# Edge values by four quarter-array products, and the picks spread over the groups anew

## Chip, cores and metric

The kernel runs on one core of one Trainium2 chip. The metric is device time of one execution in microseconds (us). Before the change it is 1745.33 us, median of three runs (1743.85 to 1745.64).

## The reference, cut to what matters

A graph with 6250 nodes and 206250 edges (sorted by destination), 64 features, 4 heads of 16:

```
Q, K, V = x @ Wq.T + bq, x @ Wk.T + bk, x @ Wv.T + bv      # per node
Ee      = edge_attr @ We.T + be                            # per edge
score   = (K[src] * Q[dst] / sqrt(16) * Ee).sum(per head)
score   = exp(clip(score, -5, 5))
out     = layernorm(x + segment_sum(V[src] * score, dst))
```

## The kernel before, in words

The edges are cut into 1612 tiles of 128, eight tiles to a **group** (202 groups, the last one of four tiles). A first part makes the K|V table (`kv_tab`) and the Q table in memory. Then one loop of 203 iterations, `for g in range(NG + 1)` (L867), handles the groups in a software pipeline whose order is written out by hand (the scheduler is off); each engine runs its own instructions in that order. What an iteration g does, by engine:

- **TensorE**, in this order: the edge product of group g + 3 (`edges`, L686), the **pick** matmuls of its share of blocks (`picks`, L654), four transposes that turn the terms of group g + 1 back to edges-by-features (`turn`, L713), two query products of group g + 2 (`queries`, L697), and, in every second iteration, 16 **sums** (`sums`, L782), which add the messages of a step of two groups by destination. All but the transposes are issued through `product` (L684), so they share that line in the profile and are told apart by their tiles: `ee` edge product, `pick` picks, `qq` queries, `room` sums.
- **ScalarE**: bias added to the edge product (`biased`, L695), exponentials (L741), two passes that make the query one-hots (L243, L249), parts of the messages (`keep`, L765).
- **VectorE**: one-hots of the picks (`hots`, L644), scores (L732 to L737), messages (L753), what `keep` left (`take`, L770), one-hots of the sums (L724), `add` (L805 and L811), which adds a finished step's sums to the result's rows, and the terms of group g + 2 (L708).
- **GpSimd**: one indirect DMA per tile that gathers the 128 source rows of `kv_tab` (L260), up to four steps ahead of use.
- **SyncE**'s queue: edge features, keys, query windows, source lists.

A **pick** stands in for gathers: the rows of four tiles at a time (a batch) are selected out of all nodes by one-hot matmuls. A batch takes 25 blocks of three matmuls (`parts` against `hot`, 512 columns), accumulated in a PSUM bank, and then a closing piece (`picked_kv`, L669: one product with the bias and four full-precision products). Two groups per batch have two of their tiles picked and not gathered. `first_unit(g)` (L74) says with which block an iteration begins: 25 blocks per three iterations from the sixth on, shared 9, 8, 8. From it follow when a batch starts (`BEGIN`), is complete (`READY`) and which groups it serves (`PICKED`, four and five groups after it is ready). `LAST`, the number of batches, is 62, so 248 tiles are picked, 40 are made by the first part, and 1324 are gathered. The picks end eleven groups before the end.

The **edge product** (L686): eight tiles lie as four pairs, `ET[g]` is 128 partitions (two tiles' 64 features) by four blocks of 128 edges. The weight `we_sb` is 128 x 128 with `We` transposed in the two diagonal quarters and zeros in the other two. One full-precision product of 512 columns fills the PSUM bank `ee`. The queries of a group are already two products with 64 output rows each, into the two partition halves of `qq`.

PSUM has eight banks here: `still` (constants), `room` (sums in 192 of 512 columns, and 64 for their total), two for picks, `ee`, `qq`, two `qe`. Messages go into `qe`. `add` stands amid the iteration (behind `take(g, 0)`) for the late steps, and at its end for all others. Most of a step's 16 sums can lie between the pairs of pick blocks, the rest behind the queries.

Of the kernel before, what the change touches and what calls it, by code (L numbers as in the profile page):

```python
# [7 lines left out]
F32 = mybir.dt.float32  # L8
# [3 lines left out]
AF = mybir.ActivationFunctionType  # L12
# [3 lines left out]
P = 128  # L16
N = 6250
C = 64
# [4 lines left out]
G = 8  # L23
# [3 lines left out]
NS = len(STEPS)  # L27
NR2 = 112
ONES = NS - 8
# [23 lines left out]
def tiles_of(g):  # L53
    return min(G, T - g * G)
# [6 lines left out]
def groups_of(s):  # L61
    return range(STEPS[s][0], STEPS[s][0] + STEPS[s][1])
# [5 lines left out]
UNITS = NB // 2  # L68
MOST = 5
LEAD = 6  # L70
# [2 lines left out]

def first_unit(g):  # L74

    return UNITS * ((g - LEAD) // 3) + (0, 9, 17)[(g - LEAD) % 3]


def when(k):
# [48 lines left out]
def tile_gnn(ctx: ExitStack, tc: tile.TileContext, x, x_blocks, by_rows, xT, wT, bias, beT, weT, eT, src, src_rows, dst,  # L128
             dst_rows, out):
    nc = tc.nc  # L130
# [29 lines left out]
    ident = consts.tile([P, P], F32, name="ident")  # L160
# [18 lines left out]
    we_sb = consts.tile([P, 2 * C], F32, name="we_sb")  # L179
# [5 lines left out]
    be_col = consts.tile([P, 1], F32, name="be_col")  # L185
# [11 lines left out]
    ET, QW, at = {}, {}, {}  # L197
    SRC, FROM, ODD, KB, TO = ({} for _ in range(5))
# [398 lines left out]
    with tc.If(rv == 0) as branch:  # L597

        with tc.tile_pool(name="work", bufs=2) as work, \
# [7 lines left out]
            nc.tensor.transpose(col, row_b[:, 0:1].to_broadcast([P, P]), ident_b)  # L607
            nc.tensor.transpose(still[:, C:C + NB].bitcast(BF16), half_b[:2 * NB].to_broadcast([2 * NB, P]),
                                ident_b[:2 * NB, :2 * NB])
            room = fixed.tile([P, 4 * P], F32, name="room")  # L610
            pa = room[:, :3 * C]
            sum_ = room[:, 3 * C:4 * C]
            px = [fixed.tile([P, 4 * P], F32, name=f"pick{k}") for k in range(2)]
            xs = [accp.tile([P, 4 * P], F32, name=f"x{k}") for k in range(2)]
            ee = fixed.tile([P, G // 2, P], F32, name="ee")
            qq = fixed.tile([P, G // 2, P], F32, name="qq")
            qe = [fixed.tile([P, G, C], F32, name=f"qe{k}") for k in range(2)]

# [30 lines left out]
            def by_two(todo):  # L649

                blocks = [(k, w, w + 1 == end) for k, end in todo for w in range(k, end)]
                return [blocks[i:i + 2] for i in range(0, len(blocks), 2)]
# [30 lines left out]
            def product(*aps, **kw):  # L683
                mark.append(nc.tensor.matmul(*aps, **kw))  # L684

            def edges(g):  # L686

                n = tiles_of(g) // 2
                product(ee[:, :n, :], we_sb, ET[g][:, :n, :], start=True, stop=True)

            def biased(g):

                n = tiles_of(g) // 2
                EB[g] = work.tile([P, G // 2, P], F32, name="eb")
                nc.scalar.activation(EB[g][:, :n], ee[:, :n], AF.Identity, bias=be_col)  # L695

            def queries(g):  # L697

                n = tiles_of(g)
                for u in range(2):  # L700
                    product(qq[u * C:(u + 1) * C, :n // 2, :], QW[g], TO[g][:, u:n:2, :],
                                     start=True, stop=True)

            def terms(g):
# [4 lines left out]

            def turn(g):  # L710

                for u in range(tiles_of(g) // 2):
                    nc.tensor.transpose(qe[g % 2][:, 2 * u:2 * u + 2, :].rearrange("p j c -> p (j c)"),  # L713
                                        TERM[g][:, u, :], ident)

            def onehot_edges(s):

# [59 lines left out]

            def pa_of(s):

                return {NS - 3: px[0][:, :3 * C], NS - 2: px[1][:, :C], NS - 1: ee[:, 0, :C]}.get(s, pa)  # L780

            def sums(s, lo=0, hi=2 * G):  # L782
                n = tiles_in(s)
                for j in range(lo, min(hi, n)):
                    product(pa_of(s), (OF if s >= WHOLE else OH)[s][:, j, :],
                            MSG[s][:, j].rearrange("p i c -> p (i c)") if s < WHOLE else MSG[s][:, j, :],
                            start=j == 0, stop=j == n - 1,
                                     skip_group_check=True)
# [78 lines left out]
            for g in range(NG + 1):  # L867
                now, before = g < NG, g > 0
                todo, ahead = pieces(g), pieces(g + 1)
                going, where = [], []  # L870
                if g < 2:
                    going = alone(lots(4)[2 * g:2 * g + 2])
                elif now and step_of[g] + KVB - 1 < NS:
                    going = lots(step_of[g] + KVB - 1)
                    going = alone(going[:2] if g == groups_of(step_of[g])[0] else going[2:])
                if g % LG == 0 and g + 3 * LG < NG:
                    fetch_edges(g // LG + 3)
                if g + 1 in BEGIN[1:]:
                    fetch_sources(BEGIN.index(g + 1) + 1, work)
                if g + 4 < NG:  # L880
                    fetch_queries(g + 4)
                if g % 2 == 0 and g + 6 < NG:
                    fetch_keys(g + 6, work)
                done = [s for s in range(NS) if groups_of(s)[-1] + 2 == g]
                parted = now and step_of[g] < WHOLE
                fetch_blocks(g)
                where.append(mark[-1])
                if g + 3 < NG:
                    edges(g + 3)
                if now:  # L890
                    products(g)
                    weigh(g)
                if g + 3 < NG:
                    biased(g + 3)
                for mc in ahead[:1]:
                    hots(*mc)
                if now:
                    message(g)
                if g + 4 < NG:
                    onehot_rows(g + 4, work.tile([3 * W, G, P], BF16, name="to", bufs=4))  # L900
                if parted:
                    keep(g, 0)
                for mc in ahead[1:]:
                    hots(*mc)
                if parted:
                    take(g, 0)
                if g > groups_of(ONES - 1)[-1]:
                    for s in done:
                        add(s)
                if g - 1 in READY:  # L910
                    picked(READY.index(g - 1))
                if g - 2 in READY:
                    picked_kv(READY.index(g - 2))
                    place_kv(READY.index(g - 2))
                where.append(mark[-1])
                summed = 0
                for i, some in enumerate(by_two(todo)):
                    picks(some)
                    if i and parted and g - 1 in ends:
                        sums(ends[g - 1], summed, summed + 4)  # L920
                        summed += 4
                    where.append(mark[-1])
                if g + 1 < NG:
                    turn(g + 1)
                if g + 2 < NG:
                    queries(g + 2)
                where.append(mark[-1])
                if g - 1 in ends and now:
                    sums(ends[g - 1], summed)
                if g + 4 < NG:  # L930
                    onehot_rows_rest(g + 4)
                if parted:
                    keep(g, 1)
                if g in BEGIN:
                    sources(BEGIN.index(g) + 1, *from_odd())
                for i, lot in enumerate(going):
                    gather((lot, where[i * len(where) // len(going)]))
                for h in ([g] if g < NG - 3 else []) + ([g + 1] if NG - 4 <= g < NG - 1 else []):
                    if h not in ends:
                        continue  # L940
                    s = ends[h]
                    t0 = STEPS[s][0] * G
                    for t in range(t0, t0 + tiles_in(s)):
                        if t and t % KEYS == 0:
                            keys(t)
                    onehot_edges(s)
                    if s >= WHOLE:
                        widen(s)
                if parted:
                    take(g, 1)  # L950
                if g <= groups_of(ONES - 1)[-1]:
                    for s in done:
                        add(s)
                if g + 2 < NG:
                    terms(g + 2)
                if done:

                    while closed < B - 2 and due[closed] <= done[-1] + 1:
                        spreads(closed)
                        closed += 1  # L960
                    if closed in BATCHES and closed > scaled:
                        roots(scaled, closed)
                        scales(scaled, closed)
                        scaled = closed
                    for _ in range(3):
                        if normed < scaled:
                            norm(normed)
                            normed += 1
# [178 lines left out]
```

## Time and profile before

| | before |
|---|---|
| median of three runs | 1745.33 us |
| profiled execution, own time | 1744.26 us |
| its span, first to last instruction | 1742.4 us |
| PE (matmul) busy | 1661.7 us, 95% |
| DVE (VectorE) busy | 1569.6 us, 90% |
| ACT (ScalarE) busy | 918.4 us, 53% |
| POOL (GpSimd) busy | 1310.5 us, 75% |
| pick matmuls (512 columns) | 4495 recorded, 1052.4 us |
| edge products | 404 records, 227.4 us |
| sums | 1592 recorded, 200.2 us |
| gathers | 1324, 1270.7 us |
| mean granted TensorE clock | 0.974 |

How to read the rows: a group's row has line, engine, operation, output<-inputs, shapes and count, then busy time in us and the mean of one in ns, then the idle time of the engine just before these instructions and what ended it. In rows in order of time, the first number is the start from the span's beginning, the second how long the merged instructions took. A matmul's record is longer than its distance to the next one, because matmuls are pipelined and the ends are modelled; so starts are compared with starts here. PEld is the weight load. POOL's busy time leaves out what its queue needs between two gathers. The chain that ended last is followed back from the last instruction, at each step to what released it.

### The profile page before, as it was taken

What the parts mean: (1) busy time and instruction counts of PE and PEld (TensorE: products, weight loads), DVE (VectorE), ACT (ScalarE), POOL (GpSimd) and SP (SyncE); (2) the same over time, 40 slices, a digit from 0 to 9 for tenths busy, and PEclk for the clock granted to TensorE, in tenths of its full rate; (3) what the DMA queues carried; (4) which work ended last, traced back from release to release, by engine and by line L of the source; (5) the groups of instructions that cost most, each with busy time, mean ns of one, the idle gap of its engine ahead of it and who ended that gap; (6) DMA issues with size and microseconds to landing.
All of it is one profiled execution on the core that took longest, in us unless ns stands there. A gap on an engine that the chain in (4) does not pass through costs nothing.

```text
span 1742.4 us, 26109 instructions
## 1 busy us (share of the span) xinstructions
PE 1661.7 (95%) x8456; PEld 881.2 (51%) x8611; DVE 1569.6 (90%) x2637; ACT 918.4 (53%) x1507; POOL 1310.5 (75%) x1374
## 2 busy tenths in 40 slices
PE   7779999999999999999999999999999999999964
PEld 6435555555555555555555555555555555555533
DVE  5689999999999999999999999999999999999976
ACT  3655555545555555555555555555555555555553
POOL 7777777777777777777777777777777777777775
PEclk9879999999999999999999999999999999999985
DMA  6744444343443443434434344344343443434331
GB/s 191 246 120 133 112 118 116 102 121 101 117 120 103 120 113 104 122 108 121 121 102 120 104 114 118 99 120 117 106 132 97 120 113 103 121 107 125 108 89 47
DMA packets 115144, 203.65 MB, mean 117 GB/s; under 512 B 55475, under 2 KB 56223, under 8 KB 114885
## 3 DMA queue, kind: packets, MB, share of 16 engines
q1 hardware_dynamic: 70914, 112.68, 21.7%
q0 software_dynamic: 43648, 88.17, 19.5%
q10 hardware_dynamic: 436, 1.04, 0.3%
q8 instruction: 69, 1.13, 0.3%
q14 instruction: 77, 0.63, 0.1%
HBM read 194.18 MB, written 7.59 MB: 116 GB/s over the span
## 4 chain that ended last, share of the span: by engine, by line
PE 90%; DMA 3%; DVE 2%; issue 2%; ACT 2%; POOL 1%; SPq 0%; POOLq 0%; DVEq 0%; ACTq 0%
PE pick L684 62%; PE ee L684 11%; PE room L684 7%; PE qe L713 5%; PE qq L684 4%; DMA kv<-kv_tab,src_i 2%; POOL kv L260 1%; PE ps L462 1%; DMA wkv<-in_wT 1%; DMA et<-in_eT 0%; PE pv L542 0%; DVE score L735 0%; DVE prod L732 0%; DVE term L708 0%; ACT eb L695 0%
## 5 line engine op out<-in xcount | busy, mean ns | idle before, releaser
L260 POOL DMA_INDIRECT kv<-kv_tab,src_i x1324 | 1270.7, 960 | 403.5 <-issue 197.1
L684 PE MATMUL pick<-hot,parts 128*128 128x512 bf16 x4495 | 1052.4, 379 | 8.3 <-issue 0.2
L684 PEld LDWEIGHTS <-parts 128*128 128x128 bf16 x4650 | 451.9, 98 | 527.1 <-issue 73.3
L644 DVE TENSOR_TENSOR hot<-from,still 128x2560 bf16<-128x2560 bf16 x366 | 460.0, 1257 | 0.0
L741 ACT ACTIVATE score<-score 128x32 f32<-128x32 f32 x202 | 46.3, 229 | 732.7 <-DVE score L737 732.7
L765 ACT ACTIVATE msg<-qe 128x512 bf16<-128x512 f32 x400 | 238.6, 596 | 35.8 <-DVE qe L753 26.9
L684 PE MATMUL ee<-et,we_sb 128*128 128x512 f32 x404 | 227.4, 645 | 7.1 <-ACT eb L695 6.1
L249 ACT ACTIVATE to<-to,one_p 126x1024 bf16<-126x1024 bf16 x198 | 226.5, 1144 | 0.0
L243 ACT ACTIVATE to<-kb,minus_row 126x1024 bf16<-126x1024 uint8 x198 | 224.6, 1134 | 0.0
L684 PE MATMUL room<-msg,of 128*128 128x192 bf16 x1592 | 200.2, 252 | 17.6 <-DVE y L811 11.3
L684 PEld LDWEIGHTS <-of 128*128 128x128 bf16 x1600 | 142.8, 100 | 109.5 <-DVE y L811 19.9
L770 DVE TENSOR_TENSOR msg<-qe,msg 128x512 bf16<-128x512 f32 x200 | 136.9, 685 | 67.4 <-ACT msg L765 61.3
L708 DVE TENSOR_TENSOR term<-eb,qq 128x512 f32<-128x512 f32 x202 | 137.0, 678 | 20.1 <-PE qq L684 15.8
L770 DVE TENSOR_TENSOR qe<-qe,msg 128x512 f32<-128x512 f32 x200 | 138.2, 691 | 18.2 <-ACT msg L765 18.2
L732 DVE TENSOR_TENSOR prod<-kv,qe 128x512 f32<-128x512 f32 x202 | 137.3, 680 | 8.2 <-DMA kv<-kv_tab,src_i 3.4
L735 DVE TENSOR_REDUCE score<-prod 128x32 f32<-128x512 f32 x202 | 138.3, 685 | 7.0
L713 PE MATMUL qe<-ident,term 128*128 128x128 f32 x806 | 126.2, 281 | 18.7 <-DVE term L708 18.7
L753 DVE TENSOR_TENSOR qe<-kv,score 128x512 f32<-128x512 f32 x200 | 139.0, 695 | 4.1 <-ACT score L741 4.1
L695 ACT ACTIVATE eb<-ee,be_col 128x512 f32<-128x512 f32 x202 | 135.1, 669 | 4.6 <-PE ee L684 4.6
L724 DVE TENSOR_TENSOR of<-still,key 128x2048 bf16<-128x2048 bf16 (+2 forms) x105 | 122.7, 1169 | 0.2
L713 PEld LDWEIGHTS qe<-ident,term 128*128 128x128 f32 x806 | 97.3, 144 | 49.8 <-DVE term L708 29.9
L684 PE MATMUL qq<-to,qw 126*64 126x512 bf16 x396 | 82.4, 413 | 0.0
(138 smaller groups left out, 855.5 us busy)
## 6 DMA issues: line engine op xcount, KB each, us to landing
et<-in_eT SPq DMA_DIRECT2D x100, 512.0 KB
kb<-key_tab SPq DMA_DIRECT2D x101, 252.0 KB
kv<-kv_tab,src_i POOLq DMA_INDIRECT x1324
srcs<-in_src_rows SPq DMA_DIRECT2D x62, 256.0 KB
qw<-q_tab SPq DMA_DIRECT2D x202, 15.8 KB
kv_tab<-kv_sb SPq DMA_DIRECT2D x4, 640.0 KB
q_tab<-q SPq DMA_DIRECT2D x5, 480.0 KB
y<-in_x_blocks SPq DMA_DIRECT2D x2, 512.0 KB
```

Source lines behind the costliest of these rows:

```text
L243: nc.scalar.activation(TO[g][:, :n, :], KB.pop(g)[:, :n * P].rearrange("p (j e) -> p j e", j=n), AF.Square, bias=minus_row3[:3 * W])
L249: nc.scalar.activation(TO[g][:, :n, :], TO[g][:, :n, :], AF.Relu, bias=one_p[:3 * W], scale=-1.0)
L260: return nc.gpsimd.indirect_dma_start(out=kv_of(g)[:, j, :], out_offset=None, in_=kv_tab[:, :], in_offset=bass.IndirectOffsetOnAxis(ap=src ...
L644: nc.vector.tensor_tensor(HOT[k][:, :hi - lo].rearrange("p b (a c) -> p b a c", c=2), pairs(FROM[m])[:, None].to_broadcast(shape), block2[ ...
L684: mark.append(nc.tensor.matmul(*aps, **kw))
L708: nc.vector.tensor_mul(TERM[g][:, :n], EB.pop(g)[:, :n], qq[:, :n])
L713: nc.tensor.transpose(qe[g % 2][:, 2 * u:2 * u + 2, :].rearrange("p j c -> p (j c)"), TERM[g][:, u, :], ident)
L732: nc.vector.tensor_mul(prod[:, :n, :], kv_of(g)[:, :n, :C], qe[g % 2][:, :n, :])
L735: nc.vector.tensor_reduce(score, prod[:, :n, :].rearrange("p g (h d) -> p g h d", h=H), axis=AX.X, op=OP.add)
L753: nc.vector.tensor_mul(to.rearrange("p g (h d) -> p g h d", h=H), kv_of(g)[:, :n, C:].rearrange("p g (h d) -> p g h d", h=H), SCORE[g][:, ...
L765: nc.scalar.activation(part, left, AF.Copy)
L770: nc.vector.tensor_sub(left if i == 0 else part_of(g, 2)[1], left, part)
```

## The change

1. **Edges.** The product over the whole array becomes four full-precision products of 64 input rows by 64 output rows, 256 columns each, one per quarter of the array: partition half `r` of `ET[g]` (one tile of each pair), tile pairs of half `u`. Output partitions are half `u`, and the two `r` go to two banks. The order is u = 0: r = 0, 1; then u = 1: r = 0, 1. The zero quarters of `we_sb` are no longer used here.
2. **Banks.** `room` becomes two banks: `ee` takes the first 256 columns of both, the sums and their total the second half of the first one. So edge values and sums share a bank, and `add` stands amid the iteration for all steps; the sums all come behind the queries, none between picks.
3. **What follows from the layout.** The bias activation reads both banks and writes the blocks interleaved; the queries take a contiguous half of the one-hots instead of every second tile; a transpose writes tiles k and k + half instead of two neighbours.
4. **Picks.** 35 blocks per four iterations. `LAST` becomes 65, so 260 tiles are picked and 1312 gathered.

```diff
 def first_unit(g):
-    return UNITS * ((g - LEAD) // 3) + (0, 9, 17)[(g - LEAD) % 3]
+    return (g - LEAD) * 35 // 4
...
-            room = fixed.tile([P, 4 * P], F32, name="room")
-            pa = room[:, :3 * C]
-            sum_ = room[:, 3 * C:4 * C]
+            room = fixed.tile([P, 2, 4 * P], F32, name="room")
+            ee = room[:, :, :2 * P].rearrange("p r (i e) -> p r i e", e=P)
+            pa = room[:, 0, 2 * P:2 * P + 3 * C]
+            sum_ = room[:, 0, 2 * P + 3 * C:2 * P + 4 * C]
...
-            ee = fixed.tile([P, G // 2, P], F32, name="ee")
...
             def edges(g):
-                n = tiles_of(g) // 2
-                product(ee[:, :n, :], we_sb, ET[g][:, :n, :], start=True, stop=True)
+                n = tiles_of(g) // 4
+                for u in range(2):
+                    for r in range(2):
+                        rows = slice(r * C, (r + 1) * C)
+                        product(ee[u * C:(u + 1) * C, r, :n, :], we_sb[rows, rows],
+                                ET[g][rows, u * n:(u + 1) * n, :], start=True, stop=True)
...
-                nc.scalar.activation(EB[g][:, :n], ee[:, :n], AF.Identity, bias=be_col)
+                nc.scalar.activation(EB[g][:, :n].rearrange("p (i r) e -> p r i e", r=2),
+                                     ee[:, :, :n // 2], AF.Identity, bias=be_col)
...
-                    product(qq[u * C:(u + 1) * C, :n // 2, :], QW[g], TO[g][:, u:n:2, :],
+                    product(qq[u * C:(u + 1) * C, :n // 2, :], QW[g],
+                                     TO[g][:, u * n // 2:(u + 1) * n // 2, :],
                                      start=True, stop=True)
...
-                for u in range(tiles_of(g) // 2):
-                    nc.tensor.transpose(qe[g % 2][:, 2 * u:2 * u + 2, :].rearrange("p j c -> p (j c)"),
-                                        TERM[g][:, u, :], ident)
+                half = tiles_of(g) // 2
+                for k in range(half):
+                    nc.tensor.transpose(qe[g % 2][:, k:k + half + 1:half, :], TERM[g][:, k, :], ident)
...
-                if g > groups_of(ONES - 1)[-1]:
-                    for s in done:
-                        add(s)
+                for s in done:
+                    add(s)
...
-                summed = 0
-                for i, some in enumerate(by_two(todo)):
+                for some in by_two(todo):
                     picks(some)
-                    if i and parted and g - 1 in ends:
-                        sums(ends[g - 1], summed, summed + 4)
-                        summed += 4
...
-                    sums(ends[g - 1], summed)
+                    sums(ends[g - 1])
...
-                if g <= groups_of(ONES - 1)[-1]:
-                    for s in done:
-                        add(s)
```

More of the change, by code (lines that the diff above doesn't have):

```diff
@@ L778, in pa_of, with sums @@
             def pa_of(s):
-                return {NS - 3: px[0][:, :3 * C], NS - 2: px[1][:, :C], NS - 1: ee[:, 0, :C]}.get(s, pa)
-            def sums(s, lo=0, hi=2 * G):
+                return {NS - 3: px[0][:, :3 * C], NS - 2: px[1][:, :C], NS - 1: room[:, 1, 2 * P:2 * P + C]}.get(s, pa)
+            def sums(s):
                 n = tiles_in(s)
-                for j in range(lo, min(hi, n)):
+                for j in range(n):
                     product(pa_of(s), (OF if s >= WHOLE else OH)[s][:, j, :],
```

## The prediction, written before the changed kernel had run

> **What bounds the kernel now.** I read the page first, then the busy time of each engine by stretches of the span, then the chain of work that ended last, cut at the same places, and last single rows of TensorE and VectorE in time.
>
> ```profile
> span 1742.4 us, 26109 instructions
> 210.00:1650.00 1440.00, 1432.45 (x7456) 742.11 (x7599) 1341.46 (x2163) 765.76 (x1218) 1093.12 (x1139) 1.00 0.41 113
> 1655.00:1732.00 77.00, 45.91 (x218) 27.39 (x217) 57.52 (x118) 36.70 (x61) 56.49 (x60) 0.72 0.28 75
> ```
>
> The columns of the last two rows are the stretch, its length, then busy time of PE, PEld, DVE, ACT and POOL, the granted clock and DMA. From 210 to 1650 us TensorE is busy 1432.45 of 1440 us: the main loop is TensorE's sum and nothing else. VectorE follows with 93%. From 1655 to 1732, the last eleven groups, which have no picks, TensorE is busy only 45.91 of 77. The chain says the same:
>
> ```profile
> by line: PE pick L684 69.9%; PE ee L684 12.0%; PE room L684 8.3%; PE qe L713 5.2%; PE qq L684 4.0%; issue 0.5%
> ...
> 1671.10 3.57 DMA kv<-kv_tab,src_i
> 1678.59 3.02 DMA kv<-kv_tab,src_i
> 1707.30 2.53 DMA kv<-kv_tab,src_i
> 1728.53 3.02 DMA kv<-kv_tab,src_i
> ```
>
> The first row is the chain between 210 and 1650: TensorE alone, 12% of it (some 173 us) edge products. The other rows are pieces after 1655: there the chain runs over gathers that landed late. GpSimd is the second limit:
>
> ```profile
> L260 POOL DMA_INDIRECT kv<-kv_tab,src_i x1139 | 1093.9, 960 | 347.1 <-issue 159.4 <-PE pick L684 63.4 <-DMA kv<-kv_tab,src_i 43.6
> L260 POOL DMA_INDIRECT kv<-kv_tab,src_i x1324: 940/944/1463, 55.6 to 1728.5; - x190
> ```
>
> In the same 1440 us it issued 1139 gathers, busy 1093.9 and idle 347.1: 1441.0 us, so 1.265 us each, the 0.30 us between two of them included, without a pause. Its last gather starts at 1728.5 and the span ends 14 us later. So TensorE sets the time up to about 1655, and GpSimd's queue, never empty, sets the last 75 us. A gain has to come in both, a loss needs only one.
>
> **The picks.** 25 blocks per three groups become 35 per four: 8.33 become 8.75 per group. In the planner's numbers 62 batches become 65, so 75 more blocks of three matmuls, three more batch ends, and 12 fewer gathers.
>
> ```profile
> 898.59 0.59 PE L684 MATMUL ee<-et,we_sb 128*128 128x512 f32 x1
> 899.11 0.39 PE L684 MATMUL pick<-bkv_p,ones_b 3*128 3x512 bf16 x1
> 899.43 1.16 PE L684 MATMUL pick<-w,x 128*128 128x128 f32 x8
> 900.42 0.38 PE L684 MATMUL pick<-hot,parts 128*128 128x512 bf16 x1
> ...
> 907.80 0.62 PE L684 MATMUL ee<-et,we_sb 128*128 128x512 f32 x1
> 908.26 0.59 PE L684 MATMUL ee<-et,we_sb 128*128 128x512 f32 x1
> 908.69 5.34 PE L684 MATMUL pick<-hot,parts 128*128 128x512 bf16 x24
> ```
>
> 24 pick matmuls take 5.34 us, the last one 0.38: (5.34 - 0.38) / 23 = 0.2157 us from one to the next. 75 x 3 x 0.2157 = 48.5 us; a batch end is 899.11 to 900.42 = 1.31 us, three are 3.9. TensorE gains **52.4 us** of work. GpSimd loses 12 x 1.265 = **15.2 us**.
>
> VectorE builds the blocks:
>
> ```profile
> L644 DVE TENSOR_TENSOR hot<-from,still 128x2560 bf16<-128x2560 bf16 x183 | 270.7, 1479 | 0.0
> ```
>
> 1.479 us for five blocks is 0.296 each, 22 us for 75. It lies behind TensorE, since VectorE has 98.5 us idle in the stretch of 1440; without that cover it would cost its 22.
>
> **The edge product.** This decides. One full-precision product is two matmul records, each with a weight load of its own, of 512 columns each. Now it becomes four products of 64 rows by 64 columns, 256 columns wide, so eight records of half the length.
>
> ```profile
> 913.87 0.60 PE L713 MATMUL qe<-ident,term 128*128 128x128 f32 x4
> 914.40 0.41 PE L684 MATMUL qq<-to,qw 126*64 126x512 bf16 x2
> 914.74 0.70 PE L684 MATMUL ee<-et,we_sb 128*128 128x512 f32 x1
> 915.27 0.59 PE L684 MATMUL ee<-et,we_sb 128*128 128x512 f32 x1
> 915.70 0.38 PE L684 MATMUL pick<-hot,parts 128*128 128x512 bf16 x1
> ...
> 914.74 0.19 PEld L684 LDWEIGHTS ee<-et,we_sb 128*128 128x128 f32 x1 [0.23 <-issue]
> 914.85 0.19 PEld L684 LDWEIGHTS ee<-et,we_sb 128*128 128x128 f32 x1
> ```
>
> Before, behind the queries: 914.74 to 915.70 = 0.96 us. Before, behind the sums (rows of 907.80 to 908.69 above): 0.89. A record streams 915.27 to 915.70 = 0.43 us; half as many columns I take at 0.214. (The eight 128-column records above, 899.43 to 900.42, come to 0.12 each, so a length does scale with columns.) The first of 914.74 took 0.53 because its weights, 0.11 from one load to the next, weren't there; 64 columns I take at 0.05. Three more rows price a change of the array's division: the query pair (64 columns each) starts 0.20 after the last transpose (913.87 + 3 x 0.11 = 914.20) where a step is 0.11, so 0.09; from the pair to the edge product, 914.40 + 0.216 = 914.62 to 914.74, is 0.12; and 898.59 to 899.11 is 0.52 instead of 0.43 ahead of the 3-row product, so 0.09.
>
> How do the eight overlap? The two query products, on two column halves, do run at once:
>
> ```profile
> L684 PE MATMUL qq<-to,qw 126*64 126x512 bf16 x394 | 81.9, 413 | 0.0
> ```
>
> Busy 81.9 us for 197 pairs is 0.416 a pair, as long as one of them. But each query product is a single record. An edge quarter is two records on the same quarter, and the rows show the second (915.27) starting only when the first has streamed. TensorE starts its matmuls in the order of the program in every row I read; if the waiting second record holds up the next quarter's first one, only neighbours overlap: quarter 1's second beside quarter 2's first, and so on. Eight records then take **five** lengths, not two: 5 x 0.214 = 1.07 us, where the old product streams four (2 x 0.43 = 0.86).
>
> The Trainium skill, page "TensorE: Matmul & The Clock Gate", section "The mechanism", states that matmuls start and end in program order and that only weight loads are pulled ahead; by that rule five lengths are right and the three later weight loads are hidden, which gives 1853 us in place of my sum below. No run here shows full-precision products in quarters.
>
> So after the queries: 0.05 + 1.07 + 0.12 to the picks' full array = 1.24, +0.28. After the sums another change, 0.10, is added: 1.34, +0.45. The groups alternate: +0.37. If the three later quarters each wait 0.05 for weights it is +0.53. I take the middle, **+0.45 us** for each of some 190 groups up to 1655: **+85 us**. Bounds: two lengths with everything at once (-0.28) and eight lengths with nothing at once (+1.01, from +0.37 + 3 x 0.214); both ends are rivals.
>
> **What costs nothing.**
>
> ```profile
> L695 ACT ACTIVATE eb<-ee,be_col 128x512 f32<-128x512 f32 x202 | 135.1, 669 | 4.6 <-PE ee L684 4.6
> ```
>
> The activation that adds the bias reads two banks and writes interleaved blocks of 128; ScalarE is busy 765.76 of 1440, so its cover is 674 us, and a 10% longer eb (0.07 of 0.67 us) would be 14 us behind it. Transposes into every second 64 columns, queries from a contiguous half, the terms: same elements, taken at nothing, between -0.05 and +0.05 a group (10 us) if addressing matters. The sums, now whole behind the queries instead of partly between picks, are the same 16 matmuls.
>
> **The new wait.** The edge values share a bank with the sums, so every second edge product waits for VectorE's add of the group before; behind it on TensorE stands everything.
>
> ```profile
> 912.84 0.69 DVE L770 TENSOR_TENSOR qe<-qe,msg 128x512 f32<-128x512 f32 x1
> ...
> 915.17 0.35 DVE L805 TENSOR_REDUCE room<-room 128x64 f32<-128x192 f32 x1
> 915.56 0.28 DVE L811 SCALAR_TENSOR_TENSOR y<-room,above,y 128x64 f32<-128x64 f32 x1
> 915.76 0.28 DVE L811 SCALAR_TENSOR_TENSOR y<-room,below,y 128x64 f32<-128x64 f32 x1
> ```
>
> The add takes 915.17 to 916.04 = 0.87 us; moved behind the subtraction that ends at 913.53 it would end at 914.40, and this edge product, after one of the shortest groups, starts at 914.74. 0.3 us are spare, more when TensorE is later: nothing in the forecast; between 0 and 0.2 us for at most 50 groups, 0 to 10 us, where TensorE is quicker.
>
> **The sum**, against the profiled execution (1744.26 us, span 1742.4): +52.4 + 85 = 137. The tail gives back: with TensorE this much later the gathers are there, and the 77 us fall towards VectorE's 57.5 plus some waits; I take -15 (-5 to -20). 1744.3 + 137.4 - 15 = 1866.7. The median of the runs lies 1.1 above the profiled one: **1868 us**, own range 1840 to 1892.
>
> **Rivals.**
> *Faster: all four quarters at once.* If TensorE holds a waiting record per quarter, the eight take two lengths: 0.05 + 0.43 + 0.12 = 0.60 after queries (-0.36), 0.70 after sums (-0.19), mean -0.275 x 190 = -52 us. That cancels the picks' +52.4, TensorE reaches the tail as now, GpSimd is 15.2 earlier: 1745.3 - 15 = 1730, up to 1740 with the new wait. It decides in favour below about -0.26 a group. For it: the query pair; against it: each quarter has two records. The Trainium skill, page "TensorEngine Tiling (Array Packing)", section "Key Properties", has tiles operating independently, loads and matmuls in parallel; by that rule this rival holds. Chance 0.30.
> *Between.* Four lengths (one more overlap): +0.16 x 190 = 30, + 52 - 15: 1813, some 1790 to 1839. 0.08.
> *The quarters take turns*, so the change doesn't do what it says: +1.01 x 190 = 192, + 52 - 15: 1975. Nothing in the rows shows two row halves at once. 0.10.
>
> **How the numbers follow.** Forecast 0.52, the others as given. Faster by over 0.2% (about what a measurement here tells from no change) needs under 1741.8: 0.28, the rival's 0.30 less 0.02 for a new wait that eats it. Within 0.2%: 0.02. Slower: 0.52 + 0.08 + 0.10 = 0.70. The range 1725 to 1892 takes in the fast rival, the one between and the forecast, 0.90 less some 0.07 for edges that I mis-size; only the turns lie outside.
>
> **What would show it.** In the changed profile, the start of a quarter's first record to the next picks: 1.2 to 1.5 us confirms, 0.6 refutes, 1.9 means turns. In single rows, does quarter 2 start with quarter 1's first or second record? TensorE busy near 100% of the loop confirms that it bounds; gathers with pauses would show GpSimd relieved. A group of pick matmuls above 0.2157 apart, or edge products idle before an add on VectorE, would make the sum wrong elsewhere.

## The result, and the profile after

The changed kernel takes 1740.78 us, median of nine runs (1739.53 to 1741.76), beside 1744.51 us (1742.83 to 1746.65) for nine runs of the kernel before: ratio 0.9975, 95% interval 0.9965 to 0.9985. So it is slightly faster, where the forecast was 1868 us, slower by 7%. It is 11 us above the figure of the rival "all four quarters at once", and it lies inside the wide range of 1725 to 1892 us only because that range took in this rival. The profiled execution takes 1741.34 us.

The page of after, first line, and the busy times by stretch (columns as before: stretch, length, PE, PEld, DVE, ACT, POOL, clock, DMA share, GB/s):

```profile
span 1739.6 us, 29016 instructions
```

```profile
210.00:1650.00 1440.00, 1430.28 (x8740) 746.53 (x8912) 1365.82 (x2207) 769.63 (x1228) 1092.81 (x1140) 1.00 0.41 113
1655.00:1732.00 77.00, 45.65 (x279) 28.48 (x278) 59.05 (x126) 38.18 (x64) 45.74 (x48) 0.71 0.24 65
```

Both stretches look as before: TensorE 1430.28 against 1432.45 us of 1440, and the last 77 us no denser, 45.65 against 45.91. In the loop only VectorE has moved, by +24 us, near the 22 that the blocks of 75 more picks were to cost. The expected +137 us of TensorE work isn't there.

Single rows of TensorE in after, in order of time (start, length, engine, line, tiles, count). The first five stand behind the sums, the last three behind the queries; the 16 sums of the first row include the one of the second:

```profile
908.67 1.49 PE L684 MATMUL room<-msg,of 128*128 128x192 bf16 x16
909.92 0.25 PE L684 MATMUL room<-msg,of 128*128 128x192 bf16 x1
910.09 0.45 PE L684 MATMUL room<-et,we_sb 64*64 64x256 f32 x4
910.36 0.40 PE L684 MATMUL room<-et,we_sb 64*64 64x256 f32 x4
910.69 0.39 PE L684 MATMUL pick<-hot,parts 128*128 128x512 bf16 x1
...
917.06 0.41 PE L684 MATMUL qq<-to,qw 126*64 126x512 bf16 x2
917.39 0.66 PE L684 MATMUL room<-et,we_sb 64*64 64x256 f32 x8
917.99 0.39 PE L684 MATMUL pick<-bkv_p,ones_b 3*128 3x512 bf16 x1
```

This is the whole disputed point. Of the eight records four start together at 910.09 (in the trace at 910.094, .101, .106 and .114), and the other four start together from 910.36. A record doesn't carry the name of its quarter; we read the four as one in each, since on the whole array a product's second record started only when the first had streamed (914.74 and 915.27 before). Two lengths, not five. From the first edge record to the picks is 0.60 us behind the sums (910.09 to 910.69) and 0.60 behind the queries (917.39 to 917.99), where before had 0.89 and 0.96. The place is typical: in the 174 groups of the loop whose eight records are all in the trace it is 0.595 us in the median (before: 0.89 behind sums, mostly 0.96 to 1.06 behind queries). The prediction's mark for "refuted" was 0.6.

The same by groups (busy us, mean ns of one | idle time ahead and what ended it):

```profile
L684 PE MATMUL pick<-hot,parts 128*128 128x512 bf16 x4689 | 1070.0, 380 | 10.1 <-issue 0.3
L684 PE MATMUL room<-et,we_sb 64*64 64x256 f32 x1608 | 139.8, 419 | 14.6 <-DVE acc L817 7.8 <-ACT to L249 4.7 <-ACT eb L699 1.8
```

The edge products have fallen from 227.4 us to 140, so they have given 87; the picks have risen by 17.6 here, where 75 x 3 x 0.2157 = 48.5 was worked out from distances. Busy times count the modelled ends of overlapping records, so neither is the balance. That is taken from one event that both kernels have, VectorE's first product of group 191, just behind the picks' end. Before and after:

```profile
1658.29 0.68 DVE L732 TENSOR_TENSOR prod<-kv,qe 128x512 f32<-128x512 f32 x1
```

```profile
1658.15 0.68 DVE L738 TENSOR_TENSOR prod<-kv,qe 128x512 f32<-128x512 f32 x1
```

0.14 us apart after 190 groups: the quarters' saving and 75 more pick blocks cancel. What is left, 84.1 us from there to the end of the span before (1742.4) and 81.4 after (1739.6), is the gain of these two executions: 2.7 us, in the tail. It comes from GpSimd. Its gathers in after, in the same 1440 us and in all (durations min/median/max in ns, first and last start):

```profile
L260 POOL DMA_INDIRECT kv<-kv_tab,src_i x1140 | 1093.5, 959 | 347.4 <-issue 147.2 <-PE pick L684 85.0 <-DMA kv<-kv_tab,src_i 48.5
```

```profile
L260 POOL DMA_INDIRECT kv<-kv_tab,src_i x1312: 938/944/1467, 55.5 to 1714.1; - x188
```

1140 in 1440 us, so GpSimd still runs without a pause, and ends 14.4 us earlier, as predicted (15.2). But that relieves next to nothing, as VectorE's waits between 1655 and 1735 us show (us in all, times, longest), before and after:

```profile
DVE qe L770 <- ACT msg L765: 10.7, 9, 1.4
...
DVE prod L732 <- DMA kv<-kv_tab,src_i: 2.5, 3, 1.3
```

```profile
DVE qe L776 <- ACT msg L771: 10.7, 9, 1.4
...
DVE prod L738 <- DMA kv<-kv_tab,src_i: 0.2, 1, 0.2
```

Before, the gathers held VectorE up for 2.5 us in the tail; after, for 0.2. Nearly all of it lay before the last two groups:

```profile
1726.52 0.69 DVE L732 TENSOR_TENSOR prod<-kv,qe 128x512 f32<-128x512 f32 x1 [1.04 <-DMA kv<-kv_tab,src_i]
...
1731.67 0.42 DVE L732 TENSOR_TENSOR prod<-kv,qe 128x256 f32<-128x256 f32 x1 [1.31 <-DMA kv<-kv_tab,src_i]
```

The chain VectorE, ScalarE, VectorE inside each group (10.7 us of waits in both) stays. So over most of the tail that chain set the pace, at about 7 us a group; the gathers ended the kernel before, but only 2 to 3 us behind it.

### The profile page after: what moved, and what is told of

Its sections match the earlier page's. It is cut to its first block, busy times and chain, and to the rows that moved or that the text cites. A ratio compares the mean times of both kernels' runs of the same rounds, so it can differ in the third digit from the quotient of the medians.

```text
span 1739.6 us, 29016 instructions
## 1 busy us (share of the span) xinstructions
PE 1653.5 (95%) x9889; PEld 882.5 (51%) x10075; DVE 1591.8 (92%) x2680; ACT 922.0 (53%) x1516; POOL 1298.6 (75%) x1362
## 4 chain that ended last, share of the span: by engine, by line
PE 83%; DVE 7%; DMA 5%; issue 2%; ACT 2%; POOL 1%; POOLq 0%; DVEq 0%; SPq 0%; ACTq 0%
PE pick L684 61%; PE room L684 13%; PE qe L720 4%; DMA kv<-kv_tab,src_i 4%; PE qq L684 3%; DVE hot L644 1%; PE ps L462 1%; POOL kv L260 1%; DVE score L741 1%; DVE prod L738 1%; DVE term L714 1%; DMA ones_tab<-ones 0%; DVE qe L759 0%; DVE qe L776 0%; DVE of L730 0%
## 5 line engine op out<-in xcount | busy, mean ns | idle before, releaser
L684 PE MATMUL pick<-hot,parts 128*128 128x512 bf16 x4689 | 1070.0, 380 | 10.1 <-issue 0.3
L684 PEld LDWEIGHTS <-parts 128*128 128x128 bf16 x4875 | 467.6, 98 | 581.1 <-issue 50.1
L644 DVE TENSOR_TENSOR hot<-from,still 128x2560 bf16<-128x2560 bf16 (+4 forms) x403 | 482.4, 1204 | 0.0
L771 ACT ACTIVATE msg<-qe 128x512 bf16<-128x512 f32 x400 | 238.5, 596 | 35.1 <-DVE qe L759 23.5
L684 PE MATMUL room<-msg,of 128*128 128x192 bf16 x1592 | 155.4, 253 | 22.9 <-DVE y L817 11.3
L684 PEld LDWEIGHTS <-of 128*128 128x128 bf16 x1600 | 132.2, 100 | 48.4 <-issue 26.6
L684 PE MATMUL room<-et,we_sb 64*64 64x256 f32 (+1 forms) x1616 | 140.5, 419 | 14.6 <-DVE acc L817 7.8
L699 ACT ACTIVATE eb<-room,be_col 128x512 f32<-128x512 f32 x202 | 135.1, 669 | 6.7 <-PE room L684 4.4
L720 PEld LDWEIGHTS qe<-ident,term 128*128 128x128 f32 x806 | 103.0, 145 | 58.1 <-DVE term L714 19.4
```

What stands on the lines that cost most here:

```text
L644: nc.vector.tensor_tensor(HOT[k][:, :hi - lo].rearrange("p b (a c) -> p b a c", c=2), pairs(FROM[m])[:, None].to_broadcast(shape), block2[ ...
L720: nc.tensor.transpose(qe[g % 2][:, k:k + half + 1:half, :], TERM[g][:, k, :], ident)
L771: nc.scalar.activation(part, left, AF.Copy)
```

## Experiments

**Theory:** the four quarters run at once, each holding its own waiting record (about -0.28 us a group of TensorE's time); this cancels the picks' work on TensorE, and the tail is worth 2 to 3 us. **Rivals:** the picks cost less than 52 us, or the quarters bring little and GpSimd's relief brings the rest; for the quarters, that records still start in one line, in an order that happened to fall well.

One thing beforehand: part of the runs fell on chips where the kernel before itself takes 2051 to 2074 us; each was compared with the kernel before there, but TensorE's records come late there, behind no wait that the profile shows (last section), so these runs can't weigh TensorE against GpSimd, and the runs that decide were made again on chips where before takes 1746 to 1748 us.

### The two parts alone, and fewer batches

`quarters_alone` is after with before's picks, `picks_alone` is before with after's, the other two are after with 64 and 63 batches:

```diff
 quarters_alone: after with
-    return (g - LEAD) * 35 // 4
+    return UNITS * ((g - LEAD) // 3) + (0, 9, 17)[(g - LEAD) % 3]
 picks_alone: before with
-    return UNITS * ((g - LEAD) // 3) + (0, 9, 17)[(g - LEAD) % 3]
+    return (g - LEAD) * 35 // 4
 batches_64: after with
+    return (g - LEAD) * 69 // 8
 batches_63: after with
+    return (g - LEAD) * 17 // 2
```

Expected of `quarters_alone`:

> The changed kernel with the old share of picks (25 blocks per three groups, 62 batches, 1324 gathers). Theory: the four quarters overlap and free TensorE of some 55 us, but GpSimd's gathers follow each other without a pause and end the kernel as before: last gather starts near 1728.5 us, TensorE idles, time 1742 to 1745 us, ratio 1.00. Rival, that the gathers are hidden and TensorE alone sets the time: about 1689 us.

Expected of `picks_alone`:

> The kernel before with 35 blocks per four groups and nothing else changed. Theory: TensorE's loop is full, so 75 more blocks and three batch ends (52 us) come on top, less 2 to 3 us in which the last groups waited for gathers: 1793 to 1797 us, ratio 1.03. Rival, that the relief of GpSimd pays: 1730 to 1741 us.

Expected of `batches_64`:

> The changed kernel with 69 blocks per eight groups: 64 batches instead of 65, 1316 gathers instead of 1312. Theory: TensorE loses 17.5 us of work and would end near 1722 us, GpSimd's last gather starts 5 us later (1719 us) and the kernel ends 14 us behind it: 1734 us, ratio 0.994, GpSimd now the bound. Rival, TensorE alone sets the time: 1723 us.

Expected of `batches_63`:

> The changed kernel with 17 blocks per two groups: 63 batches, 1320 gathers. Theory: one step further on GpSimd's side, last gather at 1724 us, time 1739 us, ratio 0.997. Rival, TensorE alone sets the time: 1706 us.

All four missed: beside 2074.22 us before, they took 2091.13 (1.0079, interval 1.0063 to 1.0094), 2064.09 (0.9954, 0.9938 to 0.9969), 2079.17 (1.0029, 1.0017 to 1.0040) and 2087.57 (1.0070, 1.0054 to 1.0086). More picks are better there and quarters worse, the reverse of the loop's balance. They settle nothing of it. The other three were run again on a chip where before takes 1746.18 us; `batches_63` was not, so its place is open.

Expected of `quarters_alone_again`:

> The changed kernel with the old share of picks, once more. Theory: GpSimd's 1324 gathers end the kernel as before, TensorE idles: 1742 to 1745 us, ratio 1.00. Rival, TensorE alone: 1689 us. Should the kernel before take 2074 us again: ratio 1.008 again.

Expected of `picks_alone_again`:

> The kernel before with 35 blocks per four groups, once more. Theory: 1793 to 1797 us, ratio 1.03. Rival, that the relief of GpSimd pays: 1730 to 1741 us. Should the kernel before take 2074 us again: ratio 0.995 again.

Expected of `batches_64_again`:

> The changed kernel with 64 batches (69 blocks per eight groups), once more, on a chip on which the kernel before should take its 1744 us. On the first chip of the experiments the kernel before took 2074 us and TensorE's instructions came late in stretches, without a wait, so that neither sum was the bound. Theory as before: GpSimd's last gather starts at 1719 us and the kernel ends 14 us later: 1734 us, ratio 0.994. Rival, TensorE alone sets the time: 1723 us. Should the kernel before take 2074 us again, the ratio is 1.003 again.

Beside 1746.18 us: quarters alone 1743.24 (0.9983, 0.9974 to 0.9993), picks alone 1795.93 (1.0282, 1.0265 to 1.0299), 64 batches 1735.23 (1734.39 to 1737.51; 0.9940, 0.9924 to 0.9957). All three within what was expected.

Picks alone, by stretch:

```profile
210.00:1650.00 1440.00, 1432.38 (x7429) 740.27 (x7569) 1321.82 (x2128) 743.68 (x1186) 1084.26 (x1120) 1.00 0.39 110
1655.00:1732.00 77.00, 70.06 (x368) 36.41 (x371) 65.05 (x106) 40.53 (x67) 40.48 (x43) 0.99 0.33 94
```

TensorE stays full past 1655 (70.06 of 77 us, before 45.91): the loop has become longer. How much longer, VectorE's first product of group 191 shows:

```profile
1711.30 0.68 DVE L732 TENSOR_TENSOR prod<-kv,qe 128x512 f32<-128x512 f32 x1
```

That is 53.0 us later than before, where the prediction had 52.4; the rest, to the end of the span at 1793.9, is 82.6 us where before had 84.1. The time rises by 49.75 us. So the picks cost what the prediction said; the first rival falls.

Quarters alone, by stretch, its gathers, VectorE's waits for gathers between 1655 and 1735, and TensorE's waits for the add between 210 and 1650:

```profile
210.00:1650.00 1440.00, 1399.11 (x8557) 730.28 (x8731) 1345.34 (x2183) 773.47 (x1231) 1091.97 (x1143) 1.00 0.40 114
```

```profile
L260 POOL DMA_INDIRECT kv<-kv_tab,src_i x1324: 940/945/1465, 55.6 to 1725.1; - x190
```

```profile
DVE prod L738 <- DMA kv<-kv_tab,src_i: 12.7, 6, 3.8
```

```profile
PE room L684 <- DVE y L817: 30.0, 26, 3.0
```

TensorE is 33 us less busy in the stretch, and the time falls by 2.9 us only: the last gather starts at 1725.1, 3.4 us earlier than before, and VectorE now waits 12.7 us for gathers. The end comes 14.7 us behind the last gather, as in the run with 64 batches below. GpSimd bounds this kernel, and that hides what the quarters save: TensorE, now ahead, waits at the shared bank for VectorE's add (30.0 us). Since GpSimd doesn't slacken (1143 gathers in 1440 us, 1.26 us each, the loop's pace before), we read that wait as TensorE's spare time and not as a bound of its own. With the picks of after, where TensorE bounds, it shows: picks alone at 1795.93, both parts at 0.9975 x 1746.18 = 1741.8, so the quarters are worth 54 us or 0.28 us for each of 190 groups (VectorE's first product of group 191 agrees: 1711.30 in picks alone, 1658.15 in after). The second rival falls too.

64 batches, by stretch, and its gathers:

```profile
210.00:1650.00 1440.00, 1424.66 (x8720) 744.23 (x8892) 1366.62 (x2223) 773.78 (x1237) 1092.68 (x1140) 1.00 0.41 114
```

```profile
L260 POOL DMA_INDIRECT kv<-kv_tab,src_i x1316: 938/944/1467, 55.7 to 1717.8; - x188
```

With 62 batches and the quarters GpSimd sets the time (1743.2), with 65 TensorE's loop does (1740.8); with 64 TensorE has a little more air (1424.66 of 1440) and the last gather still starts 10.7 us earlier than before. 0.9940 is below the 0.9975 of after, and their intervals don't touch: it beats both kernels, and is the best version found.

### The quarters' order: do records start in one line?

In both, each of the four products becomes two of 128 columns, sixteen records in all. `eight_by_quarter` finishes a quarter before the next; `eight_in_turn` goes round all quarters with the first column half, then with the second:

```diff
 eight_by_quarter: in edges of after
                     for r in range(2):
                         rows = slice(r * C, (r + 1) * C)
-                        product(ee[u * C:(u + 1) * C, r, :n, :], we_sb[rows, rows],
-                                ET[g][rows, u * n:(u + 1) * n, :], start=True, stop=True)
+                        for i in range(n):
+                            product(ee[u * C:(u + 1) * C, r, i, :], we_sb[rows, rows],
+                                    ET[g][rows, u * n + i, :], start=True, stop=True)
 eight_in_turn: the same product, with i outermost
-                for u in range(2):
-                    for r in range(2):
...
+                for i in range(n):
+                    for u in range(2):
+                        for r in range(2):
...
```

> The changed kernel with each quarter's product cut into two of 128 columns, both of a quarter issued one after the other, then the next quarter: four records of one quarter stand ahead of the next quarter's first. Theory A, a record that waits for its own quarter does not hold up the other quarters: 0.60 to 0.65 us from the first edge record to the next picks, time within 10 us of the changed kernel's 1741. Theory B, records start in the order of the program and only neighbours overlap: 13 lengths of 0.107 = 1.39, 1.5 us with what lies around it, time 1900 to 1920 us.

> The same eight products of 128 columns, issued in turn over the four quarters, twice round. Theory A: as with both of a quarter in a row, 0.60 to 0.65 us, 1741 to 1750 us. Theory B, program order with the two records of a product behind each other: 9 lengths, 1.1 us, time 1830 to 1845 us; and if the two records of neighbours are interleaved by fours, 0.60 to 0.65 us here but not with both of a quarter in a row.

One execution each, on a chip with 2074.22 us before: 2113.72 and 2115.86 us, so both missed their times. The order can still be read from rows: in the median the block takes 0.620 us by quarter and 0.600 us in turn, as expected of theory A, and by quarter the first records of two neighbouring quarters start 13 or 14 ns apart where 4 records stand from one to the next, in turn 6 or 7 ns where 2 do. So the first was run again for its time:

> Eight products of 128 columns, both of a quarter in a row, once more. Theory A, a waiting record holds up its own quarter alone: 0.62 us from the first edge record to the next picks as on the other chip, 0.025 us more than the changed kernel's in some 190 groups, 1741 to 1748 us. Theory B, program order: 1900 us or more.

That fell on such a chip again (2089.95 us, before 2051.16) and added nothing. The third, beside 1748.3 us before:

> Eight products, both of a quarter in a row, a third time. Theory A: 0.62 us a group, 1741 to 1748 us. Theory B: 1900 us or more.

1741.29 us (one execution), as theory A had it. Single rows of TensorE, the second and third inside the sixteen records:

```profile
1007.74 0.25 PE L684 MATMUL room<-msg,of 128*128 128x192 bf16 x1
1007.92 0.36 PE L684 MATMUL room<-et,we_sb 64*64 64x128 f32 x4
...
1008.19 0.42 PE L684 MATMUL room<-et,we_sb 64*64 64x128 f32 x8
...
1008.54 0.38 PE L684 MATMUL pick<-bkv_p,ones_b 3*128 3x512 bf16 x1
```

1007.92 to 1008.54 is 0.62 us. With four records of a quarter ahead of the next quarter's first in the program (taken from the source, two records to a product), the four quarters' first records still start within 40 ns of one another (0, 14, 27 and 40), then the seconds at 160 to 200, the thirds at 270 to 310 and the last at 379 to 419. The gap between quarters grows with the number of records between them, some 3 ns for each, not with their lengths. So a waiting record holds up its own quarter alone. A single line, in which the second quarter's first would start only once the first quarter's last had its turn, is excluded. Nor do the records look dealt out to the quarters in turn before they start: then the gap would be the same in both orders.

### The new wait

`add_late` puts `add` back behind the iteration for all but the late steps, so that every second edge product waits longer:

```diff
                     take(g, 0)
-                for s in done:
-                    add(s)
+                if g > groups_of(ONES - 1)[-1]:
+                    for s in done:
+                        add(s)
...
                     take(g, 1)
+                if g <= groups_of(ONES - 1)[-1]:
+                    for s in done:
+                        add(s)
```

> The changed kernel with the add of the sums back at the iteration's end for all but the late groups. Theory: every second edge product waits for it, since edge values and sums share a bank: up to 1.3 us in some 96 groups, TensorE idles ahead of edge products behind VectorE's add, 1780 to 1860 us. Rival, the add's place is free because VectorE has room: 1741 us.

2098.18 us beside 2074.22 before, on the chip that can't tell. Again, beside 1746.18:

> The changed kernel with the add at the iteration's end, once more. Theory: up to 1.3 us of waiting in some 96 groups, TensorE idle ahead of edge products behind VectorE's add, 1780 to 1860 us. Rival, the add's place is free: 1741 us.

1781.8 us (one execution), at the low end. TensorE's busy time by stretch in add_late_again, then its waits in 210 to 1650 us:

```profile
210.00:1650.00 1440.00, 1396.57 (x8507) 728.98 (x8675) 1332.17 (x2148) 749.79 (x1197) 1086.07 (x1128) 1.00 0.40 112
```

```profile
PE room L684 <- DVE y L817: 32.2, 46, 2.1
```

The same wait in after:

```profile
PE room L684 <- DVE y L817: 0.2, 1, 0.2
```

So the bank that edges and sums share is a wait of 32.2 us in 46 pieces in the stretch when the add ends late, and one of 0.2 us when it stands amid the iteration. Moving the add is a needed part of the change, worth some 40 us (1781.8 against 1741.8), and the prediction's 0 for the wait was right for the kernel it was made for. Where GpSimd holds VectorE back and TensorE runs ahead, as in quarters alone, the wait returns (30.0 us).

### The place of the sums

In after, all 16 sums stand between the queries and the edge product, which costs a change of the array's division (0.09 us, next section). `sums_first` puts them ahead of the transposes:

```diff
+                if g - 1 in ends and now:
+                    sums(ends[g - 1])
                 if g + 1 < NG:
                     turn(g + 1)
...
-                if g - 1 in ends and now:
-                    sums(ends[g - 1])
```

> The changed kernel (65 batches) with the sums issued between the picks and the transposes and not behind the queries, so that TensorE changes the array's division once less in every second group. Theory: the step from the last sum to the first edge record (0.176 us) becomes one from the last sum to the first transpose (0.083), 0.093 us in some 96 groups = 9 us off TensorE's sum: 1732 us, ratio 0.992, GpSimd (1728 us) not yet the bound. Rival, the transposes come 1.3 us later in these groups and VectorE, 95% busy, starts its scores later: 1741 us or more.

2094.99 us beside 2072.79 (1.0104, 1.0087 to 1.0121). Again:

> The sums between picks and transposes, once more, on a chip on which the kernel before should take 1745 us and not 2073. Theory: 9 us off TensorE's sum, 1732 us, ratio 0.992. Rival, VectorE starts its scores later: 1741 us or more. Should the kernel before take 2073 us again: ratio 1.010 again.

2064.88 beside 2051.16 (1.0064, 1.0041 to 1.0087); both on chips that can't tell. The third, beside 1748.3:

> The sums between picks and transposes, a third time, for a chip on which the kernel before takes 1745 us. Theory: 9 us off TensorE's sum, 1732 us, ratio 0.992. Rival, VectorE starts its scores later: 1741 us or more. Should the kernel before take over 2000 us again, the question stays open.

1746.79 us (0.9994, 0.9984 to 1.0004): no gain over before. The theory's figure missed, and the rival's held. VectorE's first product of group 191 tells where:

```profile
1653.38 0.68 DVE L738 TENSOR_TENSOR prod<-kv,qe 128x512 f32<-128x512 f32 x1
```

The loop is 4.8 us shorter than after's (the theory had 9), but the tail takes 91.4 us (to 1744.8) instead of 81.4. TensorE's sums and transposes in the tail of sums_first_third:

```profile
1691.11 1.06 PE L720 MATMUL qe<-ident,term 128*128 128x128 f32 x4
...
1700.21 1.06 PE L720 MATMUL qe<-ident,term 128*128 128x128 f32 x4
...
1709.45 1.46 PE L684 MATMUL room<-msg,of 128*128 128x192 bf16 x8 [6.76 <-DVE y L817]
...
1710.71 1.06 PE L720 MATMUL qe<-ident,term 128*128 128x128 f32 x4
```

and the transposes in the tail of after:

```profile
1695.95 1.12 PE L720 MATMUL qe<-ident,term 128*128 128x128 f32 x4
...
1702.70 1.11 PE L720 MATMUL qe<-ident,term 128*128 128x128 f32 x4
```

The transposes at 1700.21 and 1710.71 are those of the same two groups as the two of after: 10.5 us from one to the next, where after has 6.75. In this part of the tail every group is a step of its own, and its sums wait for the messages or for VectorE's add (6.76 us idle at 1709.45). Now the transposes and the queries, which feed VectorE's next group, stand behind them, and VectorE waits for the queries; between 1655 and 1735 us its waits have this line, and those of after have none like it:

```profile
DVE term L714 <- PE qq L684: 9.1, 7, 1.8
```

That is nearly all of the 10 us. It isn't the gathers: the last one starts at 1721.3, 23.5 us ahead of the end. So a gain in the loop is given back in the tail. Sums ahead in the loop alone weren't tried.

## Why the prediction was wrong, point by point

- **What bounds the kernel now**: right for the loop. Too strong for the end: "GpSimd's queue, never empty, sets the last 75 us". The chain's pieces over gathers were real, but the wait behind them was 2.5 us in 77, and the row that tells it, VectorE's wait for gathers by amount, wasn't used.
- **The picks**, +52.4 us on TensorE and 15.2 less on GpSimd: right. Measured 53.0 in the loop, +49.75 with the tail's relief in it, and the last gather 14.4 us earlier. VectorE's 22 us stayed hidden.
- **The edge product**: the step that failed is "if the waiting second record holds up the next quarter's first one, only neighbours overlap ... Eight records then take **five** lengths, not two". It took the sequence of starts seen with the whole array, where the second record needs the same cells, for a rule between quarters that share none. The runs show two lengths: a waiting record holds up its own quarter alone. Forecast +0.45 us a group, measured -0.28, which over 190 groups is 139 us; the miss is 127, since the tail was mis-sized the other way (below). The rule of the Trainium skill, page "TensorE: Matmul & The Clock Gate", section "The mechanism", that matmuls start and end in program order, was weighed for it and differs from the rows here: the second record of the first quarter stands ahead of the other quarters' first ones in the program and starts some 0.25 us behind them (910.36 against 910.10 to 910.11). The measurement decides. The other page named in the prediction, "TensorEngine Tiling (Array Packing)", section "Key Properties", on which tiles operate independently, agrees: 5 to 8 ns between quarters.
- **The price of a change of the array's division**, 0.09 to 0.12 us: right. 909.92 to 910.09 is 0.17 us where a sum's step is (909.92 - 908.67) / 15 = 0.083, so 0.09; and two lengths with these changes, the rival's 0.60, are the measured 0.60.
- **"The sums ... are the same 16 matmuls"**, taken at nothing: right for the sums themselves. The change of division between them and the quarters, 0.09 us in every second group, stands elsewhere in the forecast ("another change, 0.10, is added") and in the rival's -0.19 behind sums (0.89 - 0.60 - 0.09 = 0.20 measured).
- **The new wait**: right for this kernel, 0.2 us. That the add's place decides is shown by the 32.2 us with the add at the end.
- **The tail**, -15: mis-sized, measured -2.7, and -1.5 in picks alone (82.6 against 84.1), where TensorE is 53 us later and VectorE waits for hardly a gather any more. This is also why the fast rival, right in all its TensorE terms (-52 against some -54), gave 1730 and not 1741. With 1745.3 + 52.4 - 52 - 2.7 it would have been 1743.
- **The chances**: 0.30 for the mechanism that held, 0.52 for the one that didn't. The query pair's row, two products in the time of one, was the only row of this kernel on the question, and it spoke for the rival.

## What to carry to other kernels

A product whose weights are half zeros is worth cutting into quarters of the array: each quarter kept its own line of waiting records here, so the time was that of one quarter's records, plus a change of the array's division on either side. Where two engines bound a kernel within 1%, relief for one alone is worth almost nothing (here 2.9 us for the quarters alone, and a loss of 49.75 for the picks alone), and the best split (here 64 batches, not 62 or 65) has to be measured as a curve. Before a gain in a tail is counted, read how many microseconds the other side really waits there, not who stands in the chain.

## What the runs showed of the hardware

- The records of a quarter go into a line of that quarter; as the starts read, they are handed out in program order some 3 ns apart (13 or 14 ns for 4 records, 5 to 8 ns for 2), and start when their own quarter is free.
- On some chips the kernel before takes 2051 to 2074 us and the changed ones 2064 to 2116. There neither TensorE nor another engine is full: in the run with 64 batches TensorE is busy 1269.67 of 1440 us, where on the other chip it had 1424.66.

```profile
210.00:1650.00 1440.00, 1269.67 (x7256) 635.10 (x7399) 1148.27 (x1845) 639.78 (x1026) 922.56 (x962) 0.97 0.34 96
```

Single rows of TensorE there show idle times that end with "issue", that is, behind nothing that the profile shows:

```profile
744.77 0.66 PE L684 MATMUL room<-et,we_sb 64*64 64x256 f32 x4 [0.91 <-issue]
...
749.08 0.60 PE L684 MATMUL pick<-w,x 128*128 128x128 f32 x2 [0.83 <-issue]
...
750.55 0.61 PE L684 MATMUL pick<-hot,parts 128*128 128x512 bf16 x1 [0.87 <-issue]
```

Records came late in stretches, 0.8 to 0.9 us each, in edge products, batch ends and picks alike, and the kernels with the most records (16 for an edge product) were the slowest. The granted clock of the stretch is 0.97 there (1.00 on the other chip), too little to explain it. The DMA packets of 16 KB that carry instructions take no longer there, 0.96 us in the median where the other chip had 1.00. No run tried a cause, and it is open.
